# A four-layer graph network kernel: the check for large counts moves from ScalarE to VectorE in layer 1, and one subtraction of the layer norm from VectorE to POOL

## The chip, the cores and the metric

The kernel runs on one core of a Trainium2 chip. A core has five engines, each with its own queue of instructions, worked off in order: TensorE (PE in the profile, PEld for its weight loads), VectorE (DVE), ScalarE (ACT), GpSimd (POOL) and SyncE (SP). They wait for one another on semaphores. The metric is the device time of one execution in microseconds.

## The reference

A layer norm with relu, then four GraphSAGE layers over a graph of 6250 nodes and 100000 edges, sorted by destination, and a residual. Low destinations have many edges (they are drawn as 6250 u^2).

```python
h = jnp.maximum(_layernorm(x, axis=-1), 0.0)              # x: 6250 x 256
deg = segment_sum(ones, edge_dst)
h = _sage_mean(h, ..., W1_self, W1_neigh, b1)             # h@Ws + (segment_sum(h[src], dst)/deg)@Wn + b
h = _sage_pool(h, ..., W2_pool, b2_pool, W2_self, W2_neigh, b2)   # segment_max of relu(h@Wp + bp)
h = _sage_gcn(h, ..., W3_neigh, b3)                       # ((segment_sum + h)/(deg+1))@Wn + b
h = _sage_mean(h, ..., W4_self, W4_neigh, b4)
return x + h @ W_fc + b_fc
```

## The kernel before, in words

Nodes lie in 49 tiles (NT) of 128, edges in 782 tiles (T) of 128. Tables of node rows lie in HBM as three bf16 parts (high, middle, low), whose sum is the f32 value, so that sums over edges can be bf16 matmuls.

**Two ways to sum over edges.** For tiles of destinations with few edges each, `sums` (line 383) gathers one row for each edge by an indirect DMA from POOL into `ring` (line 401), builds a one-hot matrix of destinations, `hot`, on VectorE (397), multiplies on TensorE into the PSUM bank `pg` (419), and adds groups of four edge tiles into `acc` on VectorE (436, 438). For the first tiles, with many edges, `build` (305) makes a count matrix instead: A[source, destination], how often each source has an edge to each destination of the tile. A tile of 128 destinations is built in 16 windows of 8 destinations. For each 128 edges of a window, ScalarE makes a one-hot of the source's row in its tile, `hs`, in two steps (317, 319), VectorE a one-hot over 49 tiles x 8 destinations, `hm` (321), and TensorE multiplies them into the bank `pb`, 128x392 (327). After a window's last matmul, ScalarE reads `pb` twice: line 332 writes relu(count - 15) to a scratch tile `many` with the sum in one column of `most`, and line 334 copies the counts as fp8 into A. At a tile's end A goes to HBM (338). `dense` (446) then multiplies A with the resident rows (457).

**Large counts.** The fp8 type holds integers exactly up to 16. Line 332 finds counts above 15; lines 1264 and 1265 reduce `most` once, after layer 2's work, and set a flag that, with other checks, sends the program to a general path after layer 3 (`settle`, 58).

**Where the windows lie.** 18 tiles are built this way (HUB): tiles 0 to 7 from the layer norm's stage on and through layer 1 (128 windows, 461 edge groups), tiles 8 to 17 during layer 2.

**The prologue.** `layer_norm` (580) works on 7 groups of 7 node tiles. A group's x lies in `xt`, of which there are two buffers; `load_x` (564) of group g+2 waits for group g to leave its buffer. Statistics on VectorE (586, 587), the scale `rs` and shift `nb` on VectorE (592, 594), normalising and relu on ScalarE (596), then the split: high part by ScalarE (599), xt minus high on VectorE (600), middle part by POOL (601), low part on VectorE (602), and the store to the table `tab_h` by SP (603). Beside it run weight products (257, 261), the window keys (POOL gathers on line 711), and 45% of tile 0's build (`made.advance`, 844).

**Layer 1.** `sums` (911) runs for tiles 8 to 48, with builds and dense products of tiles 0 to 7 in between by a `Hub` (345), which spreads its list of work over the edge tiles and makes one-hots four steps ahead. As a tile is done, `done1` (865) takes a mean on ScalarE (`m`, 874), transposes on TensorE (`pt_m`, 880 and 883), copies `th` on ScalarE (885), multiplies into `pm_hp` (890, 893), and finishes `hpf` on VectorE (896) and ScalarE (897), stored by SP. PSUM has two `pb` banks and two `pg` banks in this stage.

**What sets the order.** The Python code gives the instructions of each engine in program order; a scheduler then settles the order in each queue from its own estimates of times. So an edit can also shift neighbours: in the changed program, queues differ from before only in the prologue and layer 1, and are the same, apart from the edit itself, from there on.

Of the kernel before, what the change touches and what calls it, by code (L numbers as in the profile page):

```python
# [10 lines left out]
BF16 = mybir.dt.bfloat16  # L11
# [3 lines left out]
AF = mybir.ActivationFunctionType  # L15
ALU = mybir.AluOpType
AX = mybir.AxisListType
# [3 lines left out]
P = 128  # L21
# [8 lines left out]
WIN = 8  # L30
# [48 lines left out]
def fast_path(  # L79
# [15 lines left out]
    nc = tc.nc  # L95
# [4 lines left out]
    NT = (N + P - 1) // P  # L100
# [27 lines left out]
    for d in range(NT):  # L128
        m, s = _edges_below(d * P, E, N)
        m1, s1 = _edges_below((d + 1) * P, E, N)  # L130
        lo, hi = max(0.0, m - s) if d else 0.0, m1 + s1
# [6 lines left out]
    H1, H3, H4 = HUB  # L138
    WT = P // WIN
# [79 lines left out]
    most = const.tile([P, NW], F32, name="most")  # L219
    less = const.tile([P, 1], F32, name="less")  # L220
# [18 lines left out]
    def bank(pool, tag, name, shape=None, bufs=None):  # L239
        t = pool.tile([P, FH], F32, tag=tag, name=name, **({"bufs": bufs} if bufs else {}))  # L240
        if shape is None:
            return t
        n = math.prod(shape)
        if len(shape) == 1:
            return t[:, :n]
        return t[:, :n].rearrange("p (a b) -> p a b", b=shape[1])
# [55 lines left out]
                 for i, f in enumerate(l)]  # L302
        return [f for _, _, _, f in sorted(keyed, key=lambda v: v[:3])]

    def build(d, A, keys, pool, psb):

        sk, mk, r0 = keys
        work = []
        for w in range(d * WT, (d + 1) * WT):
            hold = {}  # L310
            for k in range(k_of[w]):
                r = row_of[w, k] - r0
                hots = {}

                def hot(r=r, hots=hots):
                    t = pool.tile([P, P], BF16, name="ht", bufs=3)
                    nc.scalar.activation(t, iota_b, AF.Abs, bias=sk[:, r : r + 1])  # L317
                    hots[0] = pool.tile([P, P], BF16, name="hs", bufs=LOOK + 3)
                    nc.scalar.activation(hots[0], t, AF.Relu, bias=one, scale=-1.0)  # L319
                    hots[1] = pool.tile([P, NT * WIN], BF16, name="hm", bufs=LOOK + 3)  # L320
                    nc.vector.tensor_scalar(hots[1], iota_w, mk[:, r : r + 1], None,  # L321
                                            op0=ALU.is_equal)

                def run(k=k, w=w, hots=hots, hold=hold):
                    if k == 0:
                        hold[0] = bank(psb, "pb", "pb", (NT * WIN,))
                    nc.tensor.matmul(hold[0], hots[0], hots[1], start=(k == 0),  # L327
                                     stop=(k == k_of[w] - 1))
                    if k == k_of[w] - 1:
                        c = (w % WT) * WIN  # L330
                        many = pool.tile([P, NT * WIN], BF16, name="many", bufs=1)
                        nc.scalar.activation(many, hold[0], AF.Relu, bias=less,  # L332
                                             accum_out=most[:, w : w + 1])
                        nc.scalar.copy(A[:, :, c : c + WIN],  # L334
                                       hold[0].rearrange("p (s c) -> p s c", c=WIN),
                                       saturate=True)
                        if w % WT == WT - 1:
                            nc.sync.dma_start(tab_a[d], A.bitcast(BF16))

                work.append((hot, run))  # L340
        return work
# [193 lines left out]
    RB1 = -(-(max(row_of[w, k] for w in range(WT * H1) for k in range(k_of[w])) + 1) // P) * P  # L535
# [9 lines left out]
    with ExitStack() as pro:  # L545
# [34 lines left out]
        def layer_norm(g):  # L580
            i0 = g * LG
            xt = xts[g]
            mv = lp.tile([P, LG, 2], F32, name="mv")
            for c in range(LG):
                st = lp.tile([P, 6], F32, name="st", bufs=4)
                nc.vector.bn_stats(st, xt[:, c, :])
                nc.vector.bn_aggr(mv[:, c, :], st)
            sd = lp.tile([P, LG], F32, name="sd")
            nc.vector.tensor_scalar(sd, mv[:, :, 1], EPS, None, op0=ALU.add)
            nc.scalar.activation(sd, sd, AF.Sqrt)  # L590
            rs = lp.tile([P, LG], F32, name="rs")
            nc.vector.reciprocal(rs, sd)
            nb = lp.tile([P, LG], F32, name="nb")
            nc.vector.scalar_tensor_tensor(nb, mv[:, :, 0], -1.0, rs, op0=ALU.mult, op1=ALU.mult)
            for c in range(LG):
                nc.scalar.activation(xt[:, c, :], xt[:, c, :], AF.Relu,
                                     bias=nb[:, c : c + 1], scale=rs[:, c : c + 1])
            hi, mid, lo = (Z1[:, i0 : i0 + LG, i * FI : (i + 1) * FI] for i in range(3))
            nc.scalar.copy(hi, xt)
            nc.vector.tensor_sub(xt, xt, hi)  # L600
            nc.gpsimd.tensor_copy(mid, xt)
            nc.vector.tensor_sub(lo, xt, mid)
            nc.sync.dma_start(
                tab_h[i0 * P : (i0 + LG) * P, :].rearrange("(c p) f -> p c f", p=P),
                Z1[:, i0 : i0 + LG, :],
            )
# [96 lines left out]
        skR = ep.tile([P, RB * P - RB1], F32, name="skf")  # L703
        mkR = ep.tile([P, RB * P - RB1], F32, name="mkf")
# [150 lines left out]
    with ExitStack() as on:  # L855
# [4 lines left out]
        wk = on.enter_context(tc.tile_pool(name="fl1", bufs=2))  # L860
# [4 lines left out]
        def done1(d, acc):  # L865
# [26 lines left out]
            for k in range(KI):  # L892
# [11 lines left out]
                        lambda acc, d=d: todo.append(done1(d, acc)), extra=3)  # L904
# [102 lines left out]
    with tc.tile_pool(name="fl2c", bufs=1) as ck, ExitStack() as late:  # L1007
# [3 lines left out]
        psb = late.enter_context(tc.tile_pool(name="psb2", bufs=2, space=PSUM))  # L1011
# [4 lines left out]
        skR = ck.tile([P, RB * P - RB1], F32, name="skR")  # L1016
        mkR = ck.tile([P, RB * P - RB1], F32, name="mkR")
# [52 lines left out]
        wk = late.enter_context(tc.tile_pool(name="fl2", bufs=2))  # L1070
# [92 lines left out]
        def early_products():  # L1163
# [17 lines left out]
        steps = products2(wpool)  # L1181
        A = wk.tile([P, NT, P], F8, name="A", bufs=1)
        first, rest = (
            [w for d in ds for w in build(d, A, (skR, mkR, RB1), wk, psb)]
            for ds in (range(H1, H3), range(H3, H4))
        )
        hub = Hub(first + rest)
# [4 lines left out]
        for b in reversed(range(NB)):  # L1192
# [3 lines left out]
            for s0 in range(0, tb, G2):  # L1196
                n = min(G2, tb - s0)
                X = (xmore if at // G2 % 2 else xpool).tile([P, G2, FH], F32, name="X2")
                for k in range(n):
# [5 lines left out]
                    if s0 + k:  # L1205
                        nc.vector.scalar_tensor_tensor(  # L1206
                            X[:, k, :], prev, same[:, t : t + 1], X[:, k, :],
                            op0=ALU.mult, op1=ALU.max,
# [29 lines left out]
                if s0 + n < tb:  # L1238
# [3 lines left out]
                        op0=ALU.mult, op1=ALU.max,  # L1242
# [18 lines left out]
                    now.remove(g)  # L1261
        early.advance(len(early.work))

        nc.vector.tensor_reduce(bad[:, 3:4], most, AX.X, ALU.max)
        nc.vector.tensor_scalar(bad[:, 3:4], bad[:, 3:4], 0.0, None, op0=ALU.is_gt)

# [31 lines left out]
    with ExitStack() as on:  # L1298
# [8 lines left out]
        with tc.tile_pool(name="fl3", bufs=2) as wk:  # L1307
            def done3(d, acc):
                q = wk.tile([P, FH], F32, name="q", bufs=2)
                if d < H3:  # L1310
                    nc.vector.tensor_add(q, acc, acc3[d])
                    nc.vector.scalar_tensor_tensor(q, q, rgcn[:, d : d + 1], qrow,
                                                   op0=ALU.mult, op1=ALU.add)
                else:
                    if d in Z3:
                        z = Z3[d]
                    else:
                        z = wk.tile([P, 3 * FH], BF16, name="zown", bufs=2)
                        nc.sync.dma_start(z, tab_r[d * P : (d + 1) * P, :])
                        yield 1  # L1320
                        yield 1
                        yield 1
                    own = bank(psm, "pm", "pm_own")
                    for part in range(3):
                        nc.tensor.matmul(own, ident_b, z[:, part * FH : (part + 1) * FH],
                                         start=(part == 0), stop=(part == 2))
                    yield 1
                    nc.vector.tensor_add(acc, acc, own)
                    nc.vector.scalar_tensor_tensor(q, acc, rgcn[:, d : d + 1], qrow,
                                                   op0=ALU.mult, op1=ALU.add)  # L1330
                q3 = wk.tile([P, 3 * FO], BF16, name="q3")
                parts(q[:, FO:], FO, q3)
                nc.sync.dma_start(tab_s[d * P : (d + 1) * P, :], q3)
                nc.sync.dma_start(xq[d * P : (d + 1) * P, :], q[:, :FO])
                yield 1
                for s0, s1 in z4_early:
                    if d == s1 - 1:
                        Z4.update(resident(zk, tab_s, FO, s0, s1))
# [8 lines left out]
            for d in range(H3):  # L1347
                work += dense([s for s0, s1 in late for s in range(s0, s1)], lambda s, d=d: block(d, s), lambda s: Z3[s], FH, psd,
                              lambda acc, d=d: todo.append(done3(d, acc)))
# [3 lines left out]
        with tc.tile_pool(name="fl4", bufs=2) as wk:  # L1353
# [20 lines left out]
            for d in range(H4):  # L1374
                work += dense([s for s0, s1 in order for s in range(s0, s1)],
                              lambda s, d=d: block(d, s), lambda s: Z4[s], FO, psd,
                              lambda acc, d=d: todo.append(done4(d, acc)))
# [644 lines left out]
```

## Time and profile before

| what | us |
|---|---|
| median of 3 runs | 3401.45 (3400.34 to 3405.78) |
| the profiled execution | 3414.5 |
| its span, from first to last instruction | 3412.4 |
| busy: TensorE, VectorE, ScalarE, POOL | 2577.9, 2068.2, 1040.3, 2100.7 |
| granted TensorE clock, mean | 0.877 |
| first gather of layer 1 (line 401) | at 155.8 |
| first gather of layer 2 (line 1201) | at 1024.2 |

A row of a group of instructions reads: line, engine, operation, output<-inputs, shapes, count | busy us in all, mean ns of one | idle time of the engine just before them, and what ended most of it. "remote" or "another core or an unknown queue" is a wait whose end the trace cannot name; some matmul records are missing from it. Durations of instructions that follow at once overlap a little, so the time that one takes of its queue is read from start to start. In the instructions in order of time the columns are start, duration, engine, line, operation.

### The profile page before, as it was taken

What the parts mean: (1) busy time and instruction counts of PE and PEld (TensorE: products, weight loads), DVE (VectorE), ACT (ScalarE), POOL (GpSimd) and SP (SyncE); (2) the same over time, 40 slices, a digit from 0 to 9 for tenths busy, and PEclk for the clock granted to TensorE, in tenths of its full rate; (3) what the DMA queues carried; (4) which work ended last, traced back from release to release, by engine and by line L of the source; (5) the groups of instructions that cost most, each with busy time, mean ns of one, the idle gap of its engine ahead of it and who ended that gap; (6) DMA issues with size and microseconds to landing.
All of it is one profiled execution on the core that took longest, in us unless ns stands there. A gap on an engine that the chain in (4) does not pass through costs nothing.

```text
span 3412.4 us, 42236 instructions
## 1 busy us (share of the span) xinstructions
PE 2577.9 (76%) x12719; PEld 1431.0 (42%) x12719; DVE 2068.2 (61%) x5265; ACT 1040.3 (30%) x2959; POOL 2100.7 (62%) x2255
## 2 busy tenths in 40 slices
PE   4447777878886755578868883983688889788888
PEld 2124445545554322233333331431233333577777
DVE  7834444444437988877878887886355656333433
ACT  4836555555415787732120120100000000000000
POOL 4264555555547678877677776665566666566664
PEclk9568888889998877688989996996899999899999
DMA  5454555545559888889889998886899999777776
GB/s 172 146 136 128 153 144 148 148 139 158 163 151 290 280 271 272 271 306 299 287 285 294 291 298 276 285 270 218 322 322 347 356 348 319 247 200 202 204 209 171
DMA packets 354555, 812.52 MB, mean 238 GB/s; under 512 B 58078, under 2 KB 151494, under 8 KB 354284
## 3 DMA queue, kind: packets, MB, share of 16 engines
q0 software_dynamic: 146080, 513.65, 49.9%
q1 hardware_dynamic: 150152, 240.63, 19.4%
q10 hardware_dynamic: 58084, 55.44, 5.4%
q8 instruction: 103, 1.69, 0.2%
q14 instruction: 136, 1.11, 0.1%
HBM read 611.14 MB, written 199.17 MB: 237 GB/s over the span
## 4 chain that ended last, share of the span: by engine, by line
PE 44%; issue 14%; DMA 14%; DVE 13%; ACT 5%; POOL 5%; another core or an unknown queue 4%; SPq 0%; DVEq 0%; ACTq 0%; POOLq 0%
PE pd L457 19%; PE pg L419 11%; DVE X L1206 6%; DMA X<-rows,srcIf 5%; DMA ring<-tab_r,srcE 4%; PE pm_hp L890 4%; POOL X L1201 3%; PE pm_hp L893 2%; PE pb L327 2%; DVE X L1240 2%; PE pm_prf L1140 2%; DMA zt<-tab_r 1%; ACT hs L319 1%; ACT ht L317 1%
## 5 line engine op out<-in xcount | busy, mean ns | idle before, releaser
L1201 POOL DMA_INDIRECT X<-rows,srcIf x782 | 890.3, 1139 | 373.8 <-issue 194.1
L419 PE MATMUL pg<-ring,hot 128*128 128x256 bf16 (+2 forms) x3390 | 700.7, 317 | 142.0 <-DMA ring<-tab_r,srcE 42.6
L401 POOL DMA_INDIRECT ring<-tab_h,srcT x474 | 451.0, 951 | 402.6 <-PE pg L419 148.8
L457 PE MATMUL pd<-zt,ac 128*128 128x256 bf16 (+1 forms) x3462 | 585.3, 300 | 55.1 <-issue 38.4
L419 PEld LDWEIGHTS <-hot 128*128 128x128 bf16 x3390 | 338.0, 101 | 391.4 <-issue 197.2
L401 POOL DMA_INDIRECT ring<-tab_r,srcE x342 | 336.8, 985 | 189.0 <-PE pg L419 88.1
L457 PE MATMUL pd<-r,ae 128*128 128x512 bf16 x1536 | 372.6, 391 | 77.7 <-issue 35.0
L457 PEld LDWEIGHTS <-ac 128*128 128x128 fp8e4 x3462 | 337.7, 98 | 209.1 <-issue 83.5
L438 DVE SCALAR_TENSOR_TENSOR acc<-pg,M,acc 128x259 f32<-128x259 f32 (+2 forms) x518 | 272.1, 560 | 247.6 <-PE pg L419 173.8
L401 POOL DMA_INDIRECT ring<-tab_s,srcE x314 | 301.3, 960 | 183.5 <-PE pg L419 66.5
L327 PE MATMUL pb<-hm,hs 128*128 128x392 bf16 x781 | 264.7, 384 | 158.1 <-ACT A L334 45.3
L319 ACT ACTIVATE hs<-ht,onef 128x128 bf16<-128x128 bf16 x781 | 285.3, 399 | 204.2 <-PE pb L327 99.8
L1206 DVE SCALAR_TENSOR_TENSOR X<-X,samef 128x512 f32<-128x512 f32 x391 | 291.6, 747 | 73.6 <-DMA X<-rows,srcIf 54.4
L397 DVE TENSOR_SCALAR hot<-iota_bf,keyE 128x128 bf16<-128x128 bf16 x656 | 156.0, 268 | 271.9 <-PE pg L419 190.3
L1206 DVE SCALAR_TENSOR_TENSOR X<-X,samef,X 128x512 f32<-128x512 f32 x385 | 286.8, 745 | 29.2 <-DMA X<-rows,srcIf 24.8
L1240 DVE SCALAR_TENSOR_TENSOR X<-X,samef 128x512 f32<-128x512 f32 x385 | 287.3, 746 | 4.4
L457 PEld LDWEIGHTS <-ae 128*128 128x128 fp8e4 x1536 | 153.7, 100 | 309.5 <-issue 165.0
L332 ACT ACTIVATE many<-pb,less 128x392 bf16<-128x392 f32 x288 | 168.0, 583 | 280.8 <-PE pb L327 126.7
L321 DVE TENSOR_SCALAR hm<-iota_w,mk 128x392 bf16<-128x392 f16 x461 | 155.6, 352 | 115.0 <-PE pb L327 61.0
L1140 PE MATMUL pm_prf<-unf,hTf 128*128 128x512 f32 x392 | 203.3, 653 | 28.5 <-ACT hTf L1131 15.9
L397 DVE TENSOR_SCALAR hot<-iota_bf,keyT 128x128 bf16<-128x128 bf16 x474 | 125.0, 273 | 160.8 <-remote 59.6
L457 PE MATMUL pd<-Z,A 128*128 128x256 bf16 (+1 forms) x1176 | 200.1, 288 | 9.6 <-issue 5.0
(312 smaller groups left out, 3012.8 us busy)
## 6 DMA issues: line engine op xcount, KB each, us to landing
rows<-X SPq DMA_DIRECT2D x385, 256.0 KB
tab_r<-r SPq DMA_DIRECT2D x49, 384.0 KB
tab_a<-A SPq DMA_DIRECT2D x18, 784.0 KB
tab_t<-th SPq DMA_DIRECT2D x49, 256.0 KB
rows<-hpf SPq DMA_DIRECT2D x49, 256.0 KB
th<-tab_t ACTq DMA_DIRECT2D x49, 256.0 KB
X<-rows,srcIf POOLq DMA_INDIRECT x782
ac<-tab_a ACTq DMA_DIRECT2D x108, 112.0 KB
```

What stands on the lines that cost most here:

```text
L319: nc.scalar.activation(hots[0], t, AF.Relu, bias=one, scale=-1.0)
L327: nc.tensor.matmul(hold[0], hots[0], hots[1], start=(k == 0), stop=(k == k_of[w] - 1))
L332: nc.scalar.activation(many, hold[0], AF.Relu, bias=less, accum_out=most[:, w : w + 1])
L397: nc.vector.tensor_scalar(hot[j], iota_b, keyT[:, j - jb : j - jb + 1], None, op0=ALU.is_equal)
L401: nc.gpsimd.indirect_dma_start(out=ring[:, j % deep, :], out_offset=None, in_=table, in_offset=bass.IndirectOffsetOnAxis(ap=srcT[:, j - jb ...
L419: nc.tensor.matmul(pg[:, : F + c], hot[j], X[:, part * F : (part + 1) * F + c], start=(k == 0 and part == 2), stop=(k == n - 1 and part == 1),
L438: nc.vector.scalar_tensor_tensor(acc[d], pg, m, acc[d], op0=ALU.mult, op1=ALU.add)
L457: nc.tensor.matmul(hold[0][:, : F + c], a, z[:, part * F : (part + 1) * F + c], start=(s == ss[0] and part == 2), stop=(s == ss[-1] and pa ...
L1140: nc.tensor.matmul(pm, hT[:, c, :], un[:, c, :], start=False, stop=(c == KH - 1))
L1201: nc.gpsimd.indirect_dma_start(out=X[:, k, :], out_offset=None, in_=tab_p, in_offset=bass.IndirectOffsetOnAxis(ap=srcI[:, t : t + 1], axis=0),
L1206: nc.vector.scalar_tensor_tensor(X[:, k, :], prev, same[:, t : t + 1], X[:, k, :], op0=ALU.mult, op1=ALU.max,)
L1240: nc.vector.scalar_tensor_tensor(X[:, 0, :], prev, same[:, t : t + 1], X[:, 0, :], op0=ALU.mult, op1=ALU.max,)
```

## The change

Three edits belong together. In layer 1's builds (the prologue's part included) VectorE takes the plain maximum of each window's counts into its column of `most`, in place of ScalarE's relu(count - 15) and sum; layer 2's builds keep the ScalarE form. Before the final reduction, VectorE adds -15 (`less`) to layer 1's 128 columns, so that "greater than 0" means the same for both. And in the layer norm, POOL instead of VectorE subtracts the high part from xt, ahead of its own copy of the middle part.

```diff
-    def build(d, A, keys, pool, psb):
+    def build(d, A, keys, pool, psb, plain=True):
...
                         c = (w % WT) * WIN
-                        many = pool.tile([P, NT * WIN], BF16, name="many", bufs=1)
-                        nc.scalar.activation(many, hold[0], AF.Relu, bias=less,
-                                             accum_out=most[:, w : w + 1])
+                        if plain:
+                            nc.vector.tensor_reduce(most[:, w : w + 1], hold[0], AX.X, ALU.max)
+                        else:
+                            many = pool.tile([P, NT * WIN], BF16, name="many", bufs=1)
+                            nc.scalar.activation(many, hold[0], AF.Relu, bias=less,
+                                                 accum_out=most[:, w : w + 1])
                         nc.scalar.copy(A[:, :, c : c + WIN],
...
             nc.scalar.copy(hi, xt)
-            nc.vector.tensor_sub(xt, xt, hi)
+            nc.gpsimd.tensor_sub(xt, xt, hi)
             nc.gpsimd.tensor_copy(mid, xt)
             nc.vector.tensor_sub(lo, xt, mid)
...
-            [w for d in ds for w in build(d, A, (skR, mkR, RB1), wk, psb)]
+            [w for d in ds for w in build(d, A, (skR, mkR, RB1), wk, psb, False)]
...
+        nc.vector.tensor_scalar(most[:, : H1 * WT], most[:, : H1 * WT], less, None, op0=ALU.add)
         nc.vector.tensor_reduce(bad[:, 3:4], most, AX.X, ALU.max)
```

## The prediction

> **What bounds the kernel now.** I read the page first, then the table by stretches of time, then the groups by shape inside the stretches that the change touches, then TensorE's waits, the chain that ended last, and last the instructions in order of time around one POOL copy. The table shows where the stages lie (columns: stretch, its length, busy time and count of PE, PEld, DVE, ACT, POOL, then granted clock, DMA share, GB/s):
>
> ```profile
> 60.00:140.00 80.00, 41.55 (x122) 15.96 (x122) 78.36 (x284) 71.13 (x191) 9.47 (x5) 0.67 0.51 155
> 160.00:870.00 710.00, 528.92 (x2988) 335.30 (x2987) 306.55 (x1154) 376.59 (x1123) 378.07 (x398) 0.83 0.52 145
> ```
>
> Two different limits. From 60 to 140 us (the layer norm beside the first build) VectorE is busy 78.4 of 80 us, ScalarE 71.1, and POOL nearly idle. In layer 1 (160 to 870 us) TensorE is busiest, with a granted clock of only 0.83; VectorE has 57% of its time free and ScalarE 47%. The edits act only up to about 1000 us; the rest of the program is a dependent stage behind, whose order of instructions on each queue stays as it is, so time won or lost before 1014 us is carried to the end.
>
> In 160 to 870 us the pass that looks for large counts stands on ScalarE in this form, beside the reads of the same PSUM bank:
>
> ```profile
> L332 ACT ACTIVATE many<-pb,less 128x392 bf16<-128x392 f32 x109 | 63.3, 581 | 166.8 <-PE pb L327 71.1 <-remote 49.3 <-PE pg L419 36.4
> L332 ACT ACTIVATION_READ_ACCUMULATOR many<-pb,less 128x1 f32 x109 | 21.1, 193 | 0.0
> L890 PE MATMUL pm_hp<-Wa,th 128*128 128x512 f32 x140 | 100.6, 859 | 40.0 <-ACT th L885 29.5 <-issue 10.4
> ```
>
> ScalarE waits 167 us for a window's last matmul before this pass; that wait stays, since the copy into A waits for the same matmul. Only the pass itself goes. What TensorE waits for, the longest first, is in good part ScalarE work that queues behind it:
>
> ```profile
> PE pg L419 <- DVE acc L438: 33.8, 8, 11.1
> PE pt_m L883 <- ACT m L874: 32.4, 11, 4.4
> PE pm_hp L890 <- ACT th L885: 29.5, 16, 3.5
> ...
> PE pt_m L883 <- ACT hs L319: 8.7, 3, 3.1
> PE pt_m L883 <- ACT many L332: 6.9, 2, 4.2
> ```
>
> With the other rows of ScalarE in that answer (A, ht) this is some 90 us. The VectorE row on top is worth less than it looks: ScalarE and VectorE report waits on unknown work in the same moments (174 to 190 us), where matmul records are missing. In the chain of the same stretch the pass holds 2.8% of 710 us, 19.9 us.
>
> **ScalarE loses the pass in layer 1.** 128 windows (8 tiles of 16). The row gives 581 + 193 ns, but they overlap: at 91.49 us one starts, its read at 91.96, the copy into A at 92.05, so 0.56 us of queue each. 128 x 0.56 = 72 us of ScalarE, 109 x 0.56 = 61 of it in the stretch. Most lies beside waiting for TensorE. The part that counts is the 19.9 us on the chain. What is late next there: the copy into A (486 ns), then m, th, hs, and TensorE's own queue; I leave 20% for that and take -16 us.
>
> A second term is the clock. The th products (L890) take 859 ns where the shortest takes 592: 140 x 0.267 = 37 us of slow matmuls, just behind TensorE's waits. [...] Layer 1 together: -20 us.
>
> **VectorE gains 128 reduces.** No row has this shape. Reduces of SBUF f32 took 253 ns at 128x100 and 382 at 128x220: 1.075 ns an element, 567 at 392. PSUM copies took 313 ns at 160 and 692 at 512, which gives 563 at 392. I take 0.57 us, 0.49 of queue (pairs of the 0.48 us acc step start 0.40 apart, 0.08 less than one takes): 128 x 0.49 = 63 us. Ends 0.45 and 0.75. VectorE goes from 43% to about 51% in layer 1, so its cover is the 404 us that it idles there. The reduce adds a wait: for the window's last matmul, with hm, hot, acc and hpf queued behind it, and TensorE waiting for those. In the compiled order of the changed program the first later product of VectorE that TensorE uses lies a median of 122 TensorE rows (matmuls and weight loads) behind that matmul, under 20 in 6 of 128 windows; the same count behind the copy into A on ScalarE is 87, and behind the pass before 73. So the wait costs about nothing; ends 0 and +8. The bank is released by both readers, which now work side by side: nothing, or a slight gain within the -16.
>
> **The add at the end.** One f32 step over 128x128; a 128x160 one took 236 to 295 ns. 0.25 us in a stretch where VectorE is 79% busy, once. Nothing.
>
> **The subtraction goes from VectorE to POOL.** Seven of them, 2014 ns each on VectorE. The prologue's chain runs through the two xt buffers: load (8.9 to 10.1 us on the chain), statistics, normalising, hi, sub, mid, lo, store, next load. Three hops of it (groups 2, 4, 6) set when the first gather starts. POOL has no two-input row; the nearest is its one-input copy of the same shape, 1838 ns mean. [...] Saved on the hop: the wait in VectorE's queue, hi's end at 79.55 to sub at 80.53, 0.98. So 3.9 - 2.0 - 1.0, about +1 us per hop; with the upper end +2, with the row -1.
>
> [...]
>
> ```profile
> 82.58 0.27 DVE L321 TENSOR_SCALAR hm<-iota_w,mk 128x392 bf16<-128x392 f16 x1
> 82.61 1.79 POOL L601 CAST Z<-xt 128x1792 bf16<-128x1792 f32 x1 [18.61 <-DVE xt L600]
> 82.77 1.65 DVE L594 SCALAR_TENSOR_TENSOR nb<-mv,rs 128x7 f32<-128x7 f32 x1
> ```
>
> nb, a step of 0.16 us, takes 1.65, until the copy is over. [...] Statistics (one input, 0.4 us each) can run beside it, nb and hm cannot. [...] I add +2 us over the three hops for nb and lo that come late, and take back 1 to 2 us for the some 6 passes that leave the full ScalarE. Prologue: +3, +2, -1 and 1 for the reduces in VectorE's full stretch: +5 us; ends -3 and +15. On POOL's queue the first two subs stand in front of window gathers whose keys are used only later, and the row of gathers of layer 1 begins only after the last store to tab_h; on SP the stores and loads keep their order apart from one stash store.
>
> **Sum.** -20 + 5 = -15 us against the profiled execution, 3414.5 us (span 3412.4 and 2.1 around it): 3399.5. That execution lies 13.05 us over the median of the three runs, 3401.45, so the forecast against the median is 3386.5.
>
> **The rivals.** A measurement of this kernel can tell a change from none from about 0.2%, 6.8 us.
> (1) Nothing to see: TensorE's stalls keep their length, because A, m and th wait for the same matmuls and only the last of these counts; then a gain of 5 in layer 1 against +5 before it: 3401. For it: the 167 us that ScalarE waits ahead of the pass. Against it: the pass's 48 places on the chain.
> (2) Slower: the lock. VectorE is 98% full from 60 to 140 us. If each POOL pair (sub and copy, 5.6 us or more) stops it almost throughout, a group ends about 2.5 us later instead of 1 to 1.5, 7 x 2.5 = 17 us, and layer 1 gives back only 3: +14, 3415. It decides once the prologue grows by more than layer 1 gains, at 20 us of gain from about 2.9 us a group, at 3 us of gain from 0.4. For it: the 1.65 us of nb. Against it: only three of the seven groups lie in a row on the chain.
> [...]
>
> **How the numbers follow.** Likeliest (a gain of 7 to 28 us) 0.43, rival 1 0.17, rival 2 0.28, rival 3 0.12. Faster 0.55, same 0.17, slower 0.28. The likeliest case alone spans 3373 to 3394. The range to 3362 takes in most of rival 3, and to 3414 about half of rival 2; some 0.2 stay outside.
>
> **What would show it.** The pass gone from ScalarE below 1000 us and 128 reduces near 0.57 us on VectorE; POOL subs near 3.9 us and VectorE steps of two inputs stretched beside them; the first ring gather about 160 us instead of 155.8; layer 1's last build and the first X gather (1024.2 us before) about 15 us earlier; fewer us under m and th among TensorE's waits and a clock a little over 0.83. Wrong, if reduces make TensorE wait for acc or hm, if the first gather is later than 170 us, or if the time after 1014 us changes.

## The result and the profile after

The changed kernel takes 3425.24 us (median of 20 runs), the kernel before, measured beside it, 3415.18 (20 runs). The ratio is 1.0039, with a 95% interval of 1.0025 to 1.0053: slower by some 13 us (the medians themselves lie 10 apart). The forecast was 3386.5, with 3414 as the upper end. The profiled execution of after took 3424.96 us (span 3423.0; before 3412.4).

Two marks cut the span into stages: the first gather of layer 1 and the first gather of layer 2.

| stage (profiled executions) | before | after | forecast |
|---|---|---|---|
| up to the first gather of layer 1 (prologue) | 155.8 | 173.75 | +5 |
| from there to the first gather of layer 2 (layer 1) | 868.4 | 871.0 | -20 |
| from there to the end, unaltered | 2388.2 | 2378.3 | 0 |

So both large terms failed: the prologue grew by 18 us, and layer 1 gave nothing back. (The last stage differs by 10 us between these two executions. In e14, the same program as after, it takes 2411 us, so it says nothing of the edit.)

Where the time lies, by stretches, in after (the columns are those of the rows of before):

```profile
60.00:140.00 80.00, 45.19 (x130) 18.45 (x129) 75.18 (x261) 61.57 (x168) 23.74 (x10) 0.71 0.52 156
160.00:870.00 710.00, 521.21 (x2920) 326.32 (x2920) 350.51 (x1272) 339.74 (x935) 376.33 (x394) 0.82 0.52 145
```

In the prologue POOL is busy 23.7 us instead of 9.5. VectorE's 75.2 us look like a relief against 78.4, but the count shows 261 instructions instead of 284: it does less in the same time. In layer 1 ScalarE loses 37 us: the pass's 61 us of queue are gone, as forecast, but 25 us more of hs and ht than before lie in this stretch. VectorE takes on 44 us, the reduces' 60.6 less 17 of other work. The clock is 0.82 instead of 0.83.

The groups of layer 1 (160 to 870 us) that answer to the pass, the copy and the th products of before:

```profile
L332 DVE TENSOR_REDUCE most<-pb 128x1 f32<-128x392 f32 x108 | 60.6, 562 | 46.0 <-PE pb L327 22.3 <-remote 17.5 <-PE pg L422 5.2
L337 ACT ACTIVATE A<-pb 128x392 fp8e4<-128x392 f32 x108 | 52.2, 483 | 60.4 <-DVE hot L400 21.8 <-issue 19.9 <-DVE most L332 18.5
L893 PE MATMUL pm_hp<-Wa,th 128*128 128x512 f32 x136 | 103.2, 901 | 40.2 <-ACT th L888 33.3 <-issue 5.5 <-ACT hs L319 1.1
```

The reduce takes 562 ns (forecast 0.57 us). The copy into A now waits on VectorE: in the compiled program it waits for the reduce of the same bank (18.5 us of its idle time), so the two readers do not work side by side. The th products take 901 ns instead of 859: no clock was won.

TensorE's waits in the same stretch of after:

```profile
PE pt_m L886 <- ACT m L877: 51.2, 17, 5.9
PE pm_hp L893 <- ACT th L888: 33.3, 15, 7.3
PE pb L327 <- ACT hs L319: 15.8, 10, 6.5
...
PE pg L422 <- DVE acc L441: 12.2, 2, 7.1
```

The waits for `many` are gone, those for acc fell from 33.8 to 12.2, and those for m, th and hs grew by as much. The stalls changed their names; their sum over all rows of this view stayed about the same (181 us before, 188 after).

The prologue is read from the instructions in order of time. Five stretches of after around the second group's subtraction, of VectorE, POOL, TensorE, ScalarE and SP:

```profile
51.04 4.47 DVE L734 CAST sk<-skI 128x512 f32<-128x512 int32 x1
55.43 1.69 DVE L752 CAST rF<-rS 128x128 f32<-128x128 int32 x1
60.31 2.02 DVE L605 TENSOR_TENSOR Z<-xt,Z 128x1792 bf16<-128x1792 f32 x1
```

```profile
51.63 3.59 POOL L603 TENSOR_TENSOR xt<-xt,Z 128x1792 f32<-128x1792 f32 x1
55.28 1.76 POOL L604 CAST Z<-xt 128x1792 bf16<-128x1792 f32 x1
```

```profile
57.27 0.45 PE L755 MATMUL pt_e<-identf,rF 128*128 128x128 f32 x1 [4.98 <-DVE rF L752]
```

```profile
58.61 0.59 ACT L258 COPY wT<-pt_w 128x512 f32<-128x512 f32 x1 [15.95 <-PE pt_w L257]
```

```profile
62.39 0.37 SPq L606 DMA_DIRECT2D tab_h<-Z  x1
```

And the same steps of before:

```profile
47.62 0.42 DVE L731 CAST sk<-skI 128x512 f32<-128x512 int32 x1
47.96 0.28 DVE L749 CAST rF<-rS 128x128 f32<-128x128 int32 x1
51.59 2.02 DVE L602 TENSOR_TENSOR Z<-xt,Z 128x1792 bf16<-128x1792 f32 x1
```

```profile
53.67 0.37 SPq L603 DMA_DIRECT2D tab_h<-Z  x1
```

A cast of 0.42 us takes 4.47 and ends as POOL's subtraction does; the next one, of 0.28, takes 1.69 and ends with POOL's copy. TensorE waits 5 us for it in its own order, ScalarE behind TensorE (15.95 us instead of 8.13), and the first low part, queued on VectorE behind these key steps, is ready 8.7 us late. The first store, and the load behind it, come 8.7 us late too. Of these 8.7 us, 3.4 arose earlier, since the first cast already starts that much later (e14 says why); it also begins beside a POOL gather that is still at work (50.66 to 51.61 us). POOL's longer queue explains little here: three gathers of keys behind its first copy start 0.8 to 0.9 us later than before's, and the next one waits 5.76 us for VectorE. Later groups repeat it, with a step of the normalising chain itself under POOL's copy:

```profile
89.16 3.61 DVE L734 CAST skf<-skI 128x384 f32<-128x384 int32 x1
92.69 1.63 DVE L597 SCALAR_TENSOR_TENSOR nb<-mv,rs 128x7 f32<-128x7 f32 x1
```

POOL's pair stood at 88.39 (4.16 us) and 92.62 (1.69 us).

### The profile page after: what moved, and what is told of

Its sections match the earlier page's. It is cut to its first block, busy times and chain, and to the rows that moved or that the text cites. A ratio compares the mean times of both kernels' runs of the same rounds, so it can differ in the third digit from the quotient of the medians.

```text
span 3423.0 us, 42093 instructions
## 1 busy us (share of the span) xinstructions
PE 2575.4 (75%) x12719; PEld 1428.0 (42%) x12719; DVE 2129.1 (62%) x5387; ACT 987.6 (29%) x2703; POOL 2137.8 (62%) x2262
## 3 DMA queue, kind: packets, MB, share of 16 engines
q8 instruction: 103, 1.69, 0.2%
## 5 line engine op out<-in xcount | busy, mean ns | idle before, releaser
L1204 POOL DMA_INDIRECT X<-rows,srcIf x782 | 907.3, 1160 | 345.2 <-issue 198.4
L460 PE MATMUL pd<-r,ae 128*128 128x512 bf16 x1536 | 374.2, 393 | 76.8 <-DVE acc L1005 44.9
L319 ACT ACTIVATE hs<-ht,onef 128x128 bf16<-128x128 bf16 x781 | 292.5, 400 | 340.3 <-PE pb L327 203.6
L400 DVE TENSOR_SCALAR hot<-iota_bf,keyT 128x128 bf16<-128x128 bf16 x474 | 122.9, 272 | 122.1 <-remote 60.6
L327 PEld LDWEIGHTS <-hs 128*128 128x128 bf16 x781 | 81.2, 105 | 277.7 <-issue 127.7
L893 PE MATMUL pm_hp<-Wa,th 128*128 128x512 f32 x196 | 140.1, 853 | 61.9 <-ACT th L888 48.8
```

The lines of the kernel that those rows point to most:

```text
L400: nc.vector.tensor_scalar(hot[j], iota_b, keyT[:, j - jb : j - jb + 1], None, op0=ALU.is_equal)
L460: nc.tensor.matmul(hold[0][:, : F + c], a, z[:, part * F : (part + 1) * F + c], start=(s == ss[0] and part == 2), stop=(s == ss[-1] and pa ...
L893: nc.tensor.matmul(ph, th[:, k, :], Wa[:, k, :], start=(k == 0), stop=False)
L1204: nc.gpsimd.indirect_dma_start(out=X[:, k, :], out_offset=None, in_=tab_p, in_offset=bass.IndirectOffsetOnAxis(ap=srcI[:, t : t + 1], axis=0),
```

## The experiments

The theory after the result: (a) the prologue's loss is VectorE standing still beside POOL (called the lock here), with key steps, sd, nb and low parts behind it and other engines behind them; (b) layer 1's gain is used up by the copy's wait for the reduce. Rivals: for (a), the longer chain through POOL, or the reduces in VectorE's full stretch; for (b), a pass on ScalarE that never counted. The runs were made in five sessions, and before, measured in each, takes 3452 us in those of e1 to e4 and e13 to e15 (here called the long level, that of the first two profiles too) and 3006 to 3009 in those of e5 to e12 and e16 (the short level). So each ratio is to before in the same session, and layer 1 is compared within a level. A stage is read from one execution: the changed kernel took 871.0 and 863.7 us in layer 1 at the long level.

| run | first gather | layer 1 | ratio to before (95% interval) |
|---|---|---|---|
| before, first profile | 155.8 | 868.4 | |
| e1, subtraction alone | 167.3 | 872.6 | 1.0054 (1.0033 to 1.0074) |
| e2, reduces alone | 152.0 | 868.2 | 0.9975 (0.9954 to 0.9996) |
| e3, reduces alone, copy first | 152.2 | 874.2 | 0.9991 (0.9968 to 1.0014) |
| e4, no look for large counts | 153.4 | 876.6 | 0.9993 (0.9971 to 1.0016) |
| e5, subtraction, first two groups | 159.6 | 640.1 | 1.0037 (1.0023 to 1.0051) |
| e6, subtraction, later five | 163.9 | 643.5 | 1.0052 (1.0032 to 1.0071) |
| e7, both edits, copy first | 175.8 | 631.4 | 1.0040 (1.0023 to 1.0057) |
| e8, reduces, split on VectorE | 160.0 | 633.3 | 0.9994 (0.9975 to 1.0012) |
| e9, before again | 154.5 | 638.3 | 0.9998 (0.9982 to 1.0014) |
| e10, both, first two on VectorE | 167.7 | 631.4 | 1.0021 (1.0003 to 1.0038) |
| e11, reduces, middle part on ScalarE | 148.2 | 632.8 | 0.9963 (0.9948 to 0.9979) |
| e12, pass twice | 152.9 | 661.2 | 1.0051 (1.0031 to 1.0072) |
| e13, e11 with an idle POOL pass | 162.7 | 877.9 | 0.9994 (0.9973 to 1.0014) |
| e14, the changed kernel again | 170.3 | 863.7 | 1.0022 (1.0005 to 1.0038) |
| e15, middle part on ScalarE alone | 150.1 | 883.9 | 1.0021 (1.0004 to 1.0038) |
| e16, e11 again | 148.8 | 630.9 | 0.9948 (0.9929 to 0.9967) |

**e1_sub_only.**

```diff
-            nc.vector.tensor_sub(xt, xt, hi)
+            nc.gpsimd.tensor_sub(xt, xt, hi)
```

> The kernel before with one edit alone: POOL subtracts the high part, the check for large counts stays on ScalarE. Lock theory (VectorE stands still for the POOL subtraction and the copy behind it, and keys, nb and lo come late for the others): the first gather of layer 1 at 168 to 175 us instead of 155.8, and the whole 12 to 18 us slower than before. Rival, the prediction's price: first gather at 157 to 161, +2 to +5 us. Rival, the prologue grew because of the reduces in VectorE's full stretch: first gather within 2 us of 155.8, no change in all.

First gather 167.3 (+11.5), and 0.54% slower, 18.6 us. The edit that was forecast at +3 to +5 makes most of the loss alone, somewhat less than the 168 expected of the lock. In its trace two other key steps stand under the second group's POOL pair, and ScalarE waits for the second:

```profile
51.01 4.75 DVE L733 SCALAR_TENSOR_TENSOR mk<-mk,dwf 128x512 f32<-128x512 f32 x1
55.68 1.89 DVE L738 TENSOR_SCALAR sk<-sk 128x512 f32<-128x512 f32 x1
```

```profile
57.67 0.69 ACT L317 ACTIVATE ht<-iota_bf,sk 128x128 bf16<-128x128 bf16 x2 [5.62 <-DVE sk L738]
```

**e2_reduce_only.** The change without the subtraction (`nc.vector.tensor_sub` kept).

> The changed kernel with the subtraction back on VectorE: only the reduces are moved. Theory that the relief of ScalarE is used up because its copy into A waits for the reduce: first gather at 153 to 158 us, from there to the first gather of layer 2 866 to 872 us (868.4 before), the whole within 5 us of before. Rival, the prediction's price: that stage 20 us shorter, about 848, and the whole 14 to 20 us faster. Rival, the reduces are what lengthened the prologue: first gather above 165 us.

First gather 152.0: the prologue is 3.8 us shorter. That the passes which leave ScalarE make this is not shown; twice as many of them (e12) did not lengthen it. Layer 1 868.2: no gain. The rival that blamed the reduces for the prologue is out, and so is the forecast's -20. The whole is 8.6 us faster (1.4 to 15.9), so a few us in layer 1, which one execution cannot show, remain possible.

**e3_copy_first.** As e2, with the order of the two readers exchanged:

```diff
-                        if plain:
-                            nc.vector.tensor_reduce(most[:, w : w + 1], hold[0], AX.X, ALU.max)
                         nc.scalar.copy(A[:, :, c : c + WIN],
                                        hold[0].rearrange("p (s c) -> p s c", c=WIN),
                                        saturate=True)
+                        if plain:
+                            nc.vector.tensor_reduce(most[:, w : w + 1], hold[0], AX.X, ALU.max)
```

> As the run with the reduces alone, but the reduce comes after the copy into A in the program, so that the copy waits for the matmul alone and the reduce for the copy. If the copy's wait for the reduce eats the gain: ScalarE has no waits that a reduce ends, and the stage of layer 1 is 8 to 18 us shorter than with the reduce first (850 to 862 us), the whole 8 to 18 faster. If ScalarE's pass never counted because the next wait is for the same matmul or the clock: the stage stays within 4 us of the other. If a reduce that comes later holds up VectorE's queue or the bank: 3 to 10 us longer than the other.

Layer 1 874.2, not 850 to 862. The copy no longer waits for a reduce (the reduces wait for it instead, 13.2 us), but that gains nothing: theory (b) falls. Whether the 6 us above e2 are the cost of a later reduce or the spread of one execution, this run can't tell.

**e4_no_check.** As e2, with neither reduce nor pass in layer 1; its columns of `most` are set to 0, so large counts of tiles 0 to 7 are not looked for.

> As the run with the reduces alone, but layer 1 looks for no large counts at all (neither reduce nor pass on ScalarE; its columns are set to 0): the bound of what the relief of ScalarE can give. If the pass on ScalarE mattered and the new wait eats it: the stage of layer 1 is 12 to 22 us shorter than the 868.4 before, the whole as much faster. If the pass lay beside other waits all along: the stage is 0 to 6 us shorter. The prologue, without reduces in VectorE's full stretch, 0 to 3 us shorter in both.

Layer 1 876.6, in neither of the expected ranges: at the long level even leaving the work out gains nothing that one execution shows (the whole: -2.4 us, from -10.0 to +5.5). TensorE waits longer for m and th, though no pass stands ahead of them any more:

```profile
PE pt_m L884 <- ACT m L875: 62.8, 17, 6.5
PE pm_hp L891 <- ACT th L886: 35.0, 15, 7.3
```

With m and th at 61.9 us before and 97.8 here, this is what rival 1 of the prediction said of layer 1.

**e5_first_two and e6_later_five.** Before, with POOL's subtraction for groups 0 and 1 only, or for groups 2 to 6 only (`i0 < 2 * LG` chooses the engine).

> The kernel before with the subtraction on POOL for the first two of the seven groups only. Theory that in these two VectorE's chain of window keys stands still beside POOL and everything behind it comes late: first store to the table at 60 to 62 us instead of 53.67, first gather of layer 1 at 160 to 164, the whole +5 to +9 us. Rival, the prediction's view that these two cost nothing because nothing in the normalising chain is behind them yet: first gather within 2 us of 155.8.

> The kernel before with the subtraction on POOL for the later five groups only. If the cost is the same for each hop: first store at 53.7 us as before, each of the three hops behind it 1 to 3 us longer, first gather at 159 to 163, the whole +3 to +8. If nearly all of the loss was made in the first two groups: first gather at 155 to 158. Together with the run of the first two it should add to about the +11.5 us of the run with all seven.

First store 60.3 and first gather 159.6 in e5, 163.9 in e6: +3.8 and +8.1 against 155.8, together 11.9, against 11.5 in e1. (Against the 154.5 of e9, which ran at their level, they are 5.1 and 9.4.) So the loss is spread: the first two groups, forecast at nothing, cost 4 to 5 us at the end of the prologue (6.6 at the first store), and the later five 8 to 9, each hop from store 1 to 3 and 3 to 5 some 2 and 6 us longer than before's (36.4 and 34.4 against 34.3 and 28.6). The wholes, +11 us (7 to 15) and +16 (10 to 21), lie above what was expected (+5 to +9, +3 to +8); layer 1 is 1.9 and 5.2 us longer than e9's.

**e7_both_copy_first.** The changed kernel with the exchange of e3.

> The changed kernel with the reduce behind the copy into A in the program. Alone, the subtraction lengthened the prologue by 11.5 us and the reduces shortened it by 3.8; together +18, 10 more than their sum. If that surplus is ScalarE standing with its copy into A behind a reduce that a POOL subtraction holds up on VectorE: first gather at 162 to 168 us instead of 173.75, the whole 5 to 11 us less than the changed kernel, so +2 to +8 against before. If the surplus is only VectorE's full queue or a shifted order: first gather at 171 to 175, the whole as the changed kernel.

First gather 175.8, the whole 1.0040. The surplus of the two edits together is not the copy's wait either.

**e8_no_pool_split.** As e2, with

```diff
-            nc.gpsimd.tensor_copy(mid, xt)
+            nc.vector.tensor_copy(mid, xt)
```

> The run with the reduces alone, with the copy of the middle part moved from POOL to VectorE too, so that POOL has no pass in the layer norm. If the lock of POOL's passes costs VectorE more than the copy itself: first gather at 143 to 151 us instead of 152, the whole 1 to 9 us faster than that run and 10 to 18 faster than before. If VectorE is simply full and takes 1 to 2 us more a group: first gather at 154 to 162, the whole 2 to 10 us slower than that run.

First gather 160.0 against 152.0 of e2: the seven copies on VectorE lengthen the prologue by 8 us, more than POOL's copies with their lock. The rival's range holds.

**e9_before_again.** The kernel before.

> The kernel before, unchanged, as the reference for the stages on the same chip as the runs beside it (the two chips so far took 868 and some 640 us for layer 1). First gather at 155.8 within 1 us; layer 1 at 860 to 880 or at 636 to 648 us; the whole within the measurement of itself, ratio 1.000 within 0.003. It says how far a stage of one profiled execution can be trusted.

First gather 154.5, layer 1 638.3. The prologue of one kernel can be read to some 1.5 us here, even across the two levels (the changed kernel's less well, see e14). What differs in layer 1 is shown at the end.

**e10_both_later.** The changed kernel with the subtraction of groups 0 and 1 on VectorE.

> The changed kernel with the subtraction of the first two groups back on VectorE. Theory that the surplus of the two edits together comes from the first two groups, where a key cast of 128 columns falls under POOL's subtraction and TensorE, ScalarE and the windows wait for it: first gather at 158 to 162 us (163.9 of the later five alone, less the 3.8 that the reduces give), the whole -2 to +5 us against before. Rival, the surplus arises in the later groups, where the reduces queue on VectorE beside POOL: first gather at 167 to 172, the whole +8 to +14.

First gather 167.7, in the rival's range: the surplus does not come from the first two groups alone. The whole, +0.21% or 6.3 us, is between the two, and its stages say why: +13.2 in the prologue, -6.9 in layer 1. Its trace shows a step of the chain itself under POOL's subtraction, the variance `sd` of a later group, for which ScalarE then stood idle 3.33 us:

```profile
115.21 3.59 DVE L592 TENSOR_SCALAR sd<-mv 128x7 f32<-128x7 f32 x1
```

```profile
115.19 3.58 POOL L603 TENSOR_TENSOR xt<-xt,Z 128x1792 f32<-128x1792 f32 x1 [17.60 <-DVE mv L590]
```

In e6 a step of tile_of, which nobody waits for, stood in that place, but sd was no better off: it queued behind it and was then held by POOL's copy (from 117.41, 1.66 us). So this row shows how the lock reaches the chain, and not where the surplus comes from.

**e11_mid_scalar and e16_mid_scalar_again.** As e2, with

```diff
-            nc.gpsimd.tensor_copy(mid, xt)
+            nc.scalar.copy(mid, xt)
```

> The run with the reduces alone, with the copy of the middle part on ScalarE (1.5 to 1.7 us a group) instead of POOL, so that POOL has no pass in the layer norm and VectorE gets no new one. If POOL's lock still cost VectorE something with the copy alone: first gather at 147 to 151 us instead of 152.0, the whole 4 to 12 us faster than before. If ScalarE, which the pass has just left, is again what the chain waits for: first gather at 153 to 158, the whole within 5 us of before.

> The run with the reduces on VectorE and the middle part on ScalarE once more (no POOL pass in the layer norm), to see whether its gain depends on the chip. If the prologue's 6 to 8 us are passed on whole: first gather at 148 to 149 us and the whole 5 to 13 us faster than before on any chip. If, as with the middle part on ScalarE alone, a chip with a stalled TensorE takes it back in layer 1: first gather the same, the whole within 4 us of before or slower.

First gather 148.2 and 148.8, the whole 0.37% and 0.52% faster than before: 11 and 16 us. The copy takes 1.68 us on ScalarE, as on POOL, and no POOL pass is left in the layer norm for VectorE to stand beside. This version beats the kernel before at the short level, at which both runs fell; the changed kernel itself did not run there, and whether the gain holds at the long level was not answered.

**e12_pass_twice.** Before, with the relu pass of layer 1 issued twice in a row.

> The kernel before with ScalarE's pass over the counts done twice for every window of layer 1 (128 more passes, 72 us more of ScalarE's queue). If the pass lies beside waits for TensorE, so that leaving it out gave nothing: layer 1 at most 10 us longer, the prologue 3 to 8 us longer, the whole +3 to +15. If ScalarE's time counts in layer 1 as the chain of waits had it (a quarter to a third of each pass): layer 1 15 to 25 us longer, the whole +20 to +32.

Layer 1 661.2 against 638.3, +22.9 us for 128 passes: 0.18 us each of the 0.56 us of queue. So ScalarE's time does count when it is added, in this execution near what the chain of waits had it. The whole says less: +15 us (9 to 22), where +20 to +32 were expected. Taking the pass away gives less still: the five runs at this level with reduces (e7, e8, e10, e11, e16) lie at 630.9 to 633.3, the three with the pass (e5, e6, e9) at 638.3 to 643.5, 8.7 us between the means (6.3 against e9 alone). The prologue came out 1.6 us shorter instead of longer.

**e13_idle_pool_pass.** As e11, with a POOL pass that nobody waits for:

```diff
+            nc.gpsimd.tensor_sub(scr, hi[:, :6, :], hi[:, 1:, :])
             nc.vector.tensor_sub(xt, xt, hi)
```

> The run with the middle part on ScalarE, plus in each of the seven groups a POOL subtraction of 1536 columns between two stretches of the high part, into a tile that nobody reads: it starts where the changed kernel's subtraction starts, but nothing waits for it. It measures what POOL's pass does to the other engines alone. If the lock (VectorE standing still) makes most of the changed kernel's loss of 18 us: first gather at 157 to 167 us instead of 148.2, the whole +6 to +16 above that run. If the loss is the longer chain through POOL (3.7 us in place of 2.0, three hops and the waits): first gather at 148 to 152.

First gather 162.7 instead of 148.2: +14.5 us from seven passes of 2.8 to 4.6 us, with no data in the chain. Part of it is VectorE's own subtraction, which starts at the same moment and took 4.5 us instead of 2.0 in the last three groups; the pass itself, then VectorE's subtraction in e13 and in e11, between 40 and 150 us:

```profile
L605 POOL TENSOR_TENSOR scr<-Z 128x1536 bf16<-128x1536 bf16 x7 | 23.7, 3392 | 72.5 <-ACT Z L604 72.4
```

```profile
L606 DVE TENSOR_TENSOR xt<-xt,Z 128x1792 f32<-128x1792 f32 x7 | 21.8, 3114 | 0.0
```

```profile
L603 DVE TENSOR_TENSOR xt<-xt,Z 128x1792 f32<-128x1792 f32 x7 | 14.1, 2017 | 0.0
```

Theory (a) holds: the lock alone can make a loss of this size, though in part by a VectorE step that the changed kernel does not have.

**e14_after_again.** The changed kernel.

> The changed kernel itself, for its stages on a chip where TensorE is not held up. Prologue 172 to 175 us (+18 to +20 as before); if the relief of ScalarE is worth what the other runs there say, layer 1 5 to 10 us shorter than 638.3 (628 to 634), and the whole +9 to +14; if the copy's wait for the reduce uses the relief up, layer 1 636 to 642 and the whole +16 to +20.

First gather 170.3, layer 1 863.7, the whole +0.22%. It is the same program as after, and yet its first store is at 60.13 instead of 62.39 and its second at 65.79 instead of 70.16: under the second POOL pair stand the two steps of e1, and the cast of rF was done just before. In after one cast had been caught by the first group's copy, so everything behind it was late enough to be caught again; in e14 and in before the same cast takes 0.2 us:

```profile
45.62 2.39 DVE L721 CAST wrowf<-wrow 128x128 f32<-128x128 int32 x1
```

**e15_mid_scalar_only.** Before, with the middle part on ScalarE.

> The kernel before with the copy of the middle part on ScalarE and nothing else: the passes over the counts stay on ScalarE. It splits the gain of the run with both (first gather 148.2, layer 1 5.5 us shorter). If freeing VectorE from POOL's copy is what shortened the prologue: first gather at 149 to 153 instead of 154.5 to 155.8, the whole -2 to -6. If that needs a ScalarE freed of its passes: first gather at 155 to 161, the whole 0 to +6.

First gather 150.1, as the first case, but the whole is 0.21% slower: the prologue's gain of 4 to 6 us did not reach the end, and -2 to -6 were expected there. Layer 1 of its profile is 883.9. Why was not settled.

## Why the prediction was wrong

**The prologue: +5 forecast, +18 measured (+14.5 in e14).** The 3.9 us that the sum counts for POOL's subtraction, and its upper end, no run shows; the seven of after took 3.58 to 4.16 us, 3.69 in the mean. The term was off by 0.2 us a hop, so the loss lies elsewhere. The step that failed is "I add +2 us over the three hops for nb and lo that come late", and with it "on POOL's queue the first two subs stand in front of window gathers whose keys are used only later". Of the lock one row had been read, the 1.65 us of nb, and it was charged to two small steps, as a delay of that row. In fact six of after's seven POOL subtractions hold a VectorE step for 3.3 to 3.6 us (in the first group VectorE was idle, waiting for TensorE), and most copies the next one for up to 1.7. In a stretch where VectorE is 98% full, what stands behind the caught step is the keys, sd, nb and low parts, then ScalarE and TensorE. The first two groups alone cost 4 to 5 us (e5), the other five 8 to 9 (e6); e13 shows that a pass outside the chain can cost as much. In before itself hm took 1.48 us beside the copy at 111.61 us (1.68 us long), where a statistics step took its 0.39. The number of inputs does not tell the two kinds apart: in after casts, of one input, took 4.47 us (0.42 in before) and 3.61 (0.35).

**Layer 1: -20 forecast, +2.6 between the two profiles, -8.7 at the short level.** At the long one, the runs with the pass lie at 868.4, 872.6 and 883.9, those with reduces at 863.7 to 877.9 (mean 871.0 against 875.0): a gain of a few us at most, within the spread. The step that failed is "The part that counts is the 19.9 us on the chain", less 20% for what is late next. An added pass cost about its time on the chain (e12: 22.9 us in layer 1, though 15 in the whole, and at the other level), but a removed one gave back less. TensorE's waits for m and th took over, as e4 shows with no pass at all. The other 4 us of the -20 were for a faster clock, a term that no run shows: the granted clock came to 0.82 against 0.83, and the th products took 901 ns against 859. Rival 3 (0.12, a much faster kernel) and the range's end at 3362 rested on more of the same.

**"The bank is released by both readers, which now work side by side: nothing".** Wrong as a fact, since the copy waits for the reduce (18.5 us of ScalarE's idle time). But it cost nothing measurable in layer 1 (e3) or in the prologue (e7).

**What held.** The reduce's 0.57 us, and VectorE's share in layer 1 (49%, forecast about 51%). The reduces did not lengthen the prologue by 1 us but shortened it by 3.8 (e2), against "take back 1 to 2".

**The sum.** Of the rivals, the second came true: a prologue that grows by far more than layer 1 gives, "each POOL pair stops it almost throughout", forecast +14 and 17 of it in the prologue; measured +13 and 18. That the sizes agree so well is luck in part: the lock of the moved subtraction alone made 11.5 (e1), the rest is the surplus below. What spoke against it ("only three of the seven groups lie in a row on the chain") missed that the lock reaches what is not on the chain, and through it the chain.

**What stays open.** The two edits together cost 7 to 10 us more in the prologue than their sum (170.3 and 173.75 against 163.5). The copy's order (e7) and the first two groups (e10) do not explain it. The stores to tab_h say where it lies. The first six of e14 are within 1.1 us of e1's, so the 3.8 us that the reduces give alone are missing from the start, and its last hop, from store 6 to 7, is 1.9 us longer. After is 3.4 us later than e14 from the third store on, a difference that arises in its first two groups. That different VectorE steps are caught is seen (e14); that this makes the whole surplus was only argued.

## What to carry to other kernels

Moving a pass from a full VectorE to POOL can cost VectorE the pass's whole POOL time beside it, as here (3.3 to 3.6 us for six of seven subtractions of 3.69 in the mean). So count it as busy on both engines, and ask for each step that could be caught who waits behind it. An engine that does not stop VectorE can be the better place even when its own pass is no faster and it has little room: ScalarE took the copy in 1.68 us and was then busy 76.8 of 80 us (60 to 140 us in e11), and the seven hm steps beside the second group's copy took 1.70 us there, against 3.12 beside POOL's copy in before. A pass's share of the chain of waits was an upper bound for what removing it gave (19.9 against 8.7 us at most); only a run without it (e4) tells how much the next wait takes.

## What was not expected of the hardware

**The same program takes 13 to 15% longer in some sessions than in others.** Before takes 3415 and 3452 us in some and 3006 to 3009 in others. The session of e1 to e4 and that of e16 both ran on a chip numbered 0, one at each level, so it is not shown whether the chip or its state at the time makes the difference. Layer 1 of before takes 868.4 us in the first profile and 638.3 in e9. TensorE's waits in e9 (160 to 770 us), then the stretch itself:

```profile
PE pg L419 <- DMA ring<-tab_h,srcT: 32.3, 51, 1.7
PE pt_m L883 <- ACT m L874: 5.5, 17, 0.5
...
PE pm_hp L890 <- ACT th L885: 1.2, 6, 0.3
```

```profile
160.00:770.00 610.00, 567.38 (x3667) 378.05 (x3667) 349.87 (x1350) 409.25 (x1226) 446.64 (x470) 0.97 0.71 203
```

The granted clock is 0.97 instead of 0.83, and the long waits for m and th, 61.9 us, are 6.7. Which of the two comes first the traces do not tell. The prologues of before agree within 1.5 us (155.8 and 154.5), and a POOL subtraction takes 3.6 us at both levels (3.59 at 51.63 us in after, 3.58 at 115.19 in e10).

**Small VectorE steps are caught as well as large ones, but not every step.** A step of 128x7 elements (sd) took 3.59 us beside POOL's subtraction in e10, as long as a cast of 128x384 in after (3.61). Another of that size passed in its usual time just ahead of that cast, after the same subtraction of POOL had begun (88.39):

```profile
89.04 0.20 DVE L595 RECIPROCAL rs<-sd 128x7 f32<-128x7 f32 x1
```
